# An attention and expert kernel on one core: tokens transposed once, router logits from extra matmul columns, values projected first, one power per chunk, places and gates turned on PE

## The chip, the core and the metric

The kernel runs on one core of one Trainium2 chip. The metric is the device time of one execution in microseconds, as the median of three runs. A profiled execution gives, beside its own time, a span (first to last instruction) and a trace of every engine: PE (matrix multiply), with its weight loads shown apart as PEld, DVE (vector), ACT (scalar and activation), POOL (GpSimd) and SP (which here only starts DMAs).

## The reference

The input x has 32 rows of 256 tokens with 128 features (shape 32 x 256 x 128). With xn the normalised x (mean 0, variance 1 over the features, no weights), the result is x + attention(xn) + block(xn). All weights are float32.

```python
def attention(x):                        # 16 heads of 8, over the 256 tokens of a row
    q, k, v = heads(x @ Wq), heads(x @ Wk), heads(x @ Wv)
    qc, kc = q - q.mean(-1, keepdims=True), k - k.mean(-1, keepdims=True)
    cov = einsum('bhsd,bhtd->bhst', qc, kc) / 8
    var = jnp.var(q, -1, ddof=1)[..., :, None] * jnp.var(k, -1, ddof=1)[..., None, :] / 8
    return merge(softmax(cov + var) @ v) @ Wo

def block(x):                            # here axis 0 (32) is the sequence, axis 1 (256) the batch
    h = layernorm(x, ln1_w, ln1_b)
    q, k, v = split(h @ in_proj_w.T + in_proj_b)
    a = causal_softmax(q @ k.T / sqrt(8)) @ v          # 16 heads of 8, over 32 positions
    x1 = x + a @ out_proj_w.T + out_proj_b
    h2 = layernorm(x1, ln2_w, ln2_b)
    gates, chosen = top_k(softmax(h2 @ router_w.T), 2)  # 8 experts
    return x1 + sum over the two chosen e of gate_e * gelu(h2 @ w1[e]) @ w2[e]
```

## The kernel before, in words

All loops are written out by hand, and each engine executes its instructions in the order in which the program lists them; waits between engines follow from the tiles that instructions share. Tiles of a pool are taken in rotation: the two PSUM pools u and w have four banks each.

**First stage** (first_rounds, L454, and last_rounds, L528). The 8192 tokens are cut into 16 chunks of 512, each as four tiles of 128 tokens. A chunk is 16 groups of 32 tokens that attend to each other (the causal attention of block). Round i of the loop at L464 holds pieces of several chunks, so that each engine finds work:

- measure(i+4), L269: statistics of the tokens on DVE, then on POOL the inverse root (a pow on 128x4), the bias -mean x root, and a second pow for the second normalisation, whose factor is r2.
- norms(i+3), L288: xn on ACT into zx (four activations), then zn = zx x r2 on POOL.
- turn_in(i+2), L303: PE transposes of zx (pta), copied by ACT into xnT for the second stage, and of zn (ptb), from which ACT makes hT with the weights ln1_w and ln1_b. POOL adds the output bias to zx.
- project_in(i+2), L313: keys (pk), from which ACT makes four masked copies kb (L320, one per group of heads), queries (pq, qT), and values (pv). The values go to DRAM (vald) and come back spread out (vb, L334).
- scores(i+1), L341: into four banks of the pool w, a mask matmul (L347) each and 64 small matmuls of 32x32 (L359).
- lessened and exponents, L371 and L377: DVE subtracts the maximum, bank by bank, and ACT exponentiates two banks at a time (h = 0 at the end of round i-1, h = 1 in round i).
- turn_weights, weigh, divide, L380 to L413: PE transposes the probabilities (ptp, to pT), multiplies them with the values (po), and DVE divides by the sums.
- turn_out and project_out, L415 and L419: transposes of the result (pto, oT), output projection px, x1 on DVE, statistics of x1, and on POOL the inverse root and the sum x + x1, which goes to DRAM (resd).
- normalise(i-1), L433: zx becomes the normalised x1 (POOL). turn_normed(i-2), L440, transposes it (ptc) and ACT makes h with ln2_w and ln2_b; logits(i-2), L444, multiplies h with the router (pl), and DVE copies the result to lg.

In rounds 3 to 5 set_second clears tiles of the second stage on POOL.

**Second stage** (step, L942). For each of 32 rows of 256 tokens, in two halves of the heads (64 units u, eight heads each), two heads per step: project (L554) multiplies 128 tokens of xnT, taken with a stride of 32 elements, with the three weight matrices (pp, 384 columns), ACT squares and copies, turn_qk transposes, scores_of (L594) computes scores twice, as sm for the row maxima (DVE, L622) and as sT for the exponentials (ACT, L625), weigh_head multiplies with the values, and divide_lessen, turn and close finish the row. A generator, route (L717), runs beside it: it yields after each of its instructions, and the step loop takes one to three of them at a time (L992): softmax, the two largest gates, the place of each token in its expert's blocks, then 128 indirect DMAs on POOL that scatter the tokens (L801). Places and gates are needed again by row; they are written to DRAM and read back in the other order (L792 to L798). In the middle of the stage the 71 expert blocks run (L870), and combine (L894) gathers their results during the second half.

Of the kernel before, what the change touches and what calls it, by code (L numbers as in the profile page):

```python
# [68 lines left out]
def block_kernel(  # L69
# [26 lines left out]
    xv = x.rearrange("s (i c k) e -> i c s (k e)", c=4, k=4)  # L96
# [7 lines left out]
    xnT = cp.tile([P, NCHUNK, 512], F32, name="xnT")  # L104
# [11 lines left out]
    posd = dp.tile([NB, SEQ, 2], I32, name="posd")  # L116
    gated = dp.tile([NB, SEQ, 2], F32, name="gated")
    xsd_views = dram_disjoint_views(xsd, 2 * NTILE)
    rv = resd.rearrange("s (i c k) e -> i c s (k e)", c=4, k=4)

    vec = cp.tile([P, 7], F32, name="vec")
    l1w, l1b, l2w, l2b = (vec[:, n:n + 1] for n in range(4))
# [5 lines left out]
    mhalf = cp.tile([P, 4, 1], F32, name="mhalf")  # L128
    wqkv = cp.tile([P, 3, P], F32, name="wqkv")
    wo = cp.tile([P, P], F32, name="wo")  # L130
    inT = cp.tile([P, 3, P], F32, name="inT")
    outT = cp.tile([P, P], F32, name="outT")
    rT = cp.tile([P, NE], F32, name="rT")

# [5 lines left out]
    def load(i):  # L140
        xt = ax.tile([P, 4, P], F32, tag="xt", name=f"xt{i}")
        for c in range(4):
            nc.sync.dma_start(xt[32 * c:32 * c + 32].rearrange("s k e -> s (k e)"), xv[i, c])
        return xt
# [13 lines left out]
    late = xnT[:, NCHUNK - 2:NCHUNK].rearrange("p i t -> p (i t)").rearrange("p (n m) -> p n m", m=P)  # L158
    ipw, opw, qkw, rw, bvs = late[:, 0:3], late[:, 3], late[:, 4:6], late[0:NE, 6], late[:, 7]
    qkT, ccen = zx[:, NTILE - 2:NTILE], zx[:, NTILE - 3]  # L160

    def loads():
# [7 lines left out]
        nc.scalar.dma_start(opw, out_proj_w)  # L170
        nc.scalar.dma_start(bout, out_proj_b.partition_broadcast(P))
# [3 lines left out]
        nc.sync.dma_start(rw, router_w)  # L175
# [5 lines left out]
    def set_in():  # L181
        nc.vector.tensor_scalar(bk4, cst[:, C_M4:C_M4 + 4], bk, None, ALU.mult)
        pt = bank_u([P, 4, P], "pt0")
        for n in range(3):
            nc.tensor.transpose(pt[:, n, :], ipw[:, n, :], ident)
        nc.tensor.transpose(pt[:, 3, :], opw, ident)
        nc.vector.tensor_copy(inT[:, 0:2, :], pt[:, 0:2, :])

        nc.vector.tensor_copy(
            inT[:, 2, :].rearrange("p (j g d) -> p j g d", j=4, g=4),  # L190
            pt[:, 2, :].rearrange("p (g j d) -> p j g d", j=4, g=4),
        )
        nc.vector.tensor_copy(outT, pt[:, 3, :])


        nc.vector.tensor_copy(bvs, bv.to_broadcast([P, P]))
        pbo = bank_u([P, P], "pbo")
        nc.tensor.matmul(pbo, bvs, outT, start=True, stop=True)
        nc.vector.tensor_tensor(bout, bout, pbo, ALU.add)

    def set_rest():
        pt = bank_w([P, 4, P], "pt1")
        nc.tensor.transpose(pt[:, 0, :], qkw[:, 0, :], ident)
        nc.tensor.transpose(pt[:, 1, :], qkw[:, 1, :], ident)
        nc.tensor.transpose(pt[:, 2, 0:NE], rw, ident[0:NE, 0:NE])
        nc.vector.tensor_copy(qkT, pt[:, 0:2, :])
        nc.vector.tensor_copy(rT, pt[:, 2, 0:NE])
# [3 lines left out]
        nc.vector.tensor_copy(wqkv[:, 0:2, :], pb)  # L211

# [29 lines left out]

    def set_values(n):
        nc.gpsimd.memset(vs[n].rearrange("p j k g d -> p (j k g) d")[:, :, HD:HD + 1], 1.0)
        nc.gpsimd.memset(vbs[n], 0.0)
# [9 lines left out]
    xts, rss, nrm, mvs, zns, hTs, qTs, kbt, scs, prs, pTs, wps, os, oTs, x1s, h2s = ({} for _ in range(16))  # L255

    def stats(src, tag, i, bufs=2):

        st = a2.tile([P, 4, 6], F32, tag="st", name=f"st{tag}{i}")
        mv = a2.tile([P, 4, 2], F32, tag=f"mv{tag}", name=f"mv{tag}{i}")  # L260
# [3 lines left out]
        rs = a2.tile([P, 4, 1], F32, tag=f"rs{tag}", name=f"rs{tag}{i}")  # L264
        nc.gpsimd.tensor_scalar(rs, mv[:, :, 1:2], EPS, None, ALU.add)
        nc.gpsimd.tensor_tensor(rs, rs, mhalf, ALU.pow)
        return mv, rs

    def measure(i):  # L269


        mv, rs = stats(xts[i], "a", i)
        nb = a2.tile([P, 4, 1], F32, tag="nb", name=f"nb{i}")
        nc.gpsimd.tensor_tensor(nb, mv[:, :, 0:1], rs, ALU.mult)
        nc.gpsimd.tensor_scalar(nb, nb, -1.0, None, ALU.mult)
        r2 = a2.tile([P, 4, 1], F32, tag="r2", name=f"r2{i}")
        nc.gpsimd.tensor_tensor(r2, rs, rs, ALU.mult)
        nc.gpsimd.tensor_tensor(r2, r2, mv[:, :, 1:2], ALU.mult)
        nc.gpsimd.tensor_scalar(r2, r2, EPS, None, ALU.add)
        nc.gpsimd.tensor_tensor(r2, r2, mhalf, ALU.pow)  # L280
        nrm[i] = rs, nb, r2
# [6 lines left out]
    def norms(i):  # L288
        rs, nb, r2 = nrm.pop(i)
        for k in range(4):  # L290
            nc.scalar.activation(
                tokens(i)[:, k, :], xts[i][:, k, :], AF.Identity, bias=nb[:, k, :], scale=rs[:, k, :]
            )
# [9 lines left out]
    def turn_in(i):  # L303

        nc.scalar.copy(
            xnT[:, i, :].rearrange("p (c k s) -> p k c s", c=4, k=4),
            transposed(tokens(i), "a", i).rearrange("p (k c s) -> p k c s", k=4, c=4),
        )
        hTs[i] = a2.tile([P, 512], F32, tag="hT", name=f"hT{i}")
        nc.scalar.activation(hTs[i], transposed(zns.pop(i), "b", i), AF.Identity, bias=l1b, scale=l1w)  # L310
        nc.gpsimd.tensor_tensor(tokens(i), tokens(i), bout.unsqueeze(1).to_broadcast([P, 4, P]), ALU.add)

    def project_in(i):  # L313
        hT = hTs.pop(i)
        pk = bank_w([P, 512], f"pk{i}")
        nc.tensor.matmul(pk, inT[:, 1, :], hT, start=True, stop=True)  # L316
# [5 lines left out]
        nc.tensor.matmul(pq, inT[:, 0, :], hT, start=True, stop=True)  # L322
        qTs[i] = a2.tile([P, 512], F32, tag="qT", name=f"qT{i}")
        nc.scalar.activation(qTs[i], pq, AF.Identity, bias=bq, scale=1.0)
        pv = bank_u([P, 4, 4, 32], f"pv{i}")
        for k in range(4):
            nc.tensor.matmul(pv[:, :, k, :], hT[:, k * P:(k + 1) * P], inT[:, 2, :], start=True, stop=True)
        nc.scalar.copy(
            vs[i % 2].rearrange("p j k g d -> p (j k g) d")[:, :, 0:HD],
            pv.rearrange("p j k (g d) -> p (j k g) d", d=HD),  # L330
        )
        nc.sync.dma_start(vald[i], vs[i % 2].rearrange("p j k g d -> p j (k g d)"))
# [86 lines left out]
    def project_out(i):  # L419

        oT = oTs.pop(i)
        px = bank_w([P, 4, P], f"px{i}")
        for k in range(4):
            nc.tensor.matmul(px[:, k, :], oT[:, k * P:(k + 1) * P], outT, start=True, stop=True)  # L424
        x1 = x1s[i] = a2.tile([P, 4, P], F32, tag="x1", name=f"x1{i}")
        nc.vector.tensor_tensor(x1, px, tokens(i), ALU.add)
        mvs[i], rss[i] = stats(x1, "c", i)
        xt = xts.pop(i)
        nc.gpsimd.tensor_tensor(xt, xt, x1, ALU.add)
        for c in range(4):  # L430
            nc.sync.dma_start(rv[i, c], xt[32 * c:32 * c + 32].rearrange("s k e -> s (k e)"))

    def normalise(i, eng=nc.gpsimd):  # L433
        x1, mv, rs = x1s.pop(i), mvs.pop(i), rss.pop(i)
        for k in range(4):
# [4 lines left out]
    def turn_normed(i):  # L440
        h2s[i] = a2.tile([P, 512], F32, tag="h2", name=f"h2{i}")
        nc.scalar.activation(h2s[i], transposed(tokens(i), "c", i), AF.Identity, bias=l2b, scale=l2w)

    def logits(i):  # L444
        pl = bank_u([P, 4, NE], f"pl{i}")
        h2 = h2s.pop(i)
        for k in range(4):
            nc.tensor.matmul(pl[:, k, :], h2[:, k * P:(k + 1) * P], rT, start=True, stop=True)
        nc.vector.tensor_copy(lg[:, 4 * i:4 * i + 4, :], pl)
# [4 lines left out]
    def first_rounds():  # L454
        loads()
        nc.vector.memset(mhalf, -0.5)
        measure(0)
        nc.gpsimd.tensor_copy(identb, ident)
        nc.gpsimd.tensor_copy(causalb, cst[:, C_CAUSAL:C_CAUSAL + 32])
        norms(0)  # L460
        set_in()
        measure(1)
        set_values(0)
        for i in range(-2, NCHUNK):  # L464
# [21 lines left out]
            if chunk(i + 2):  # L486
                project_in(i + 2)
            if i == NCHUNK - 1:
                project(0, 0)
# [6 lines left out]
            if i == -2:  # L496
                set_rest()
                set_values(1)
                nc.gpsimd.memset(zero, 0.0)
            if 3 <= i < 3 + NV:  # L500
                set_second(i - 3)
            if chunk(i + 3):
                norms(i + 3)
            if chunk(i + 4):
                measure(i + 4)
# [3 lines left out]
            if chunk(i - 1):  # L509
                normalise(i - 1)  # L510
            if chunk(i + 1):
                scores(i + 1)
            if chunk(i - 2):
                turn_normed(i - 2)
# [10 lines left out]
            if chunk(i - 2):  # L525
                logits(i - 2)

    def last_rounds():  # L528
# [5 lines left out]
        yield turn_normed(n - 1)  # L534
        yield project_out(n)
        yield logits(n - 1)
        yield normalise(n, nc.vector)
        yield turn_normed(n)
        yield logits(n)
# [5 lines left out]
    xs_all = xnT.rearrange("p i (b s) -> p (i b) s", s=NB)  # L545
    NU = 2 * NB
    pps = {}
    ot, qas, kas, exs, pos, oas, res = {}, {}, {}, {}, {}, {}, {}
# [5 lines left out]
    def project(s, ti):  # L554
# [3 lines left out]
            pp.rearrange("p n m -> p (n m)"), xs_all[:, ti * P:(ti + 1) * P, s],  # L558
# [4 lines left out]
        nc.scalar.activation(sq, pqk, AF.Square, scale=1.0 / math.sqrt(HD - 1))  # L563
        qk = qkts[s % NQ][:, ti].rearrange("p n g m r -> p (n g m) r")
        nc.scalar.copy(qk[:, :, 0:HD], pqk)
        pps[s, ti] = pp, sq

    def project_rest(s, ti):
# [4 lines left out]
        nc.scalar.copy(vo[:, :, 0, 0:8], pi[:, :, 0])  # L573
        qk = qkts[s % NQ][:, ti].rearrange("p n g m r -> p (n g m) r")
        nc.vector.tensor_reduce(qk[:, :, HD:HD + 1], sq, AX.X, ALU.add)
        nc.vector.tensor_copy(vo[:, :, 1, 8:16], pi[:, :, 1])
# [139 lines left out]

    def route():  # L717
# [3 lines left out]
        oh1, oh2 = r_tile("oh1", NTILE, NE), r_tile("oh2", NTILE, NE)  # L721
        yield nc.vector.tensor_reduce(m, lg, AX.X, ALU.max)
# [61 lines left out]
        yield nc.vector.tensor_tensor(a, a, n8[:, 0:1, :].to_broadcast(all8), ALU.add)  # L784
        posi = r_tile("posi", NTILE, 2, dt=I32)
# [235 lines left out]
```

## Time and profile before

| | |
|---|---|
| median of 3 runs | 991.37 us (991.09 to 992.39) |
| the profiled execution | 992.8 us, its span 991.0 us |
| mean granted clock of PE in it | 0.976 of full speed |
| busy in the span | PE 940.2, PEld 679.0, DVE 706.3, ACT 655.1, POOL 561.9 us |
| first stage | to about 285 us |
| second stage, first half; experts; second half | about 290 to 565; 565 to 705; 705 to 986 us |

The page gives the span in 40 equal slices, with the busy share of each engine in tenths and the clock that PE was granted. Lines of groups read: line, engine, operation, output from input, shapes, count; busy us, mean ns of one; idle time of the engine before them, and what ended it. Lines of the timeline read: start in us, length, engine, line, operation, tiles, shapes, count, and in brackets an idle time and its releaser. PE's instructions overlap, so that the distance between starts is what one costs in a row of them. A float32 matmul is two instructions, a transposition one.

### The profile page before, as it was taken

The page shows a single profiled execution, that of the slowest core. Times are in us where ns is not written, and L with a number is a line of the kernel's source. Part 1 is how long each engine was busy: PE and PEld are TensorE (multiplying, and loading weights), DVE is VectorE, ACT ScalarE, POOL GpSimd, SP SyncE. Part 2 cuts the span into 40 slices and gives each one's busy share as a digit, 9 for nine tenths or more (in the row PEclk, how much of TensorE's full clock was granted, in tenths as well). Part 3 has the DMA queues.
Part 4 walks back from the last instruction along what each step waited for, and adds up shares of the span by engine and source line. Part 5 has one row for each costly group of instructions (what it writes and reads, how often), then busy time and mean ns, then how long its engine had stood idle before and what let it go on. Part 6 is the DMA issues. An engine that isn't in the chain of part 4 may idle for free.

```text
span 991.0 us, 32300 instructions
## 1 busy us (share of the span) xinstructions
PE 940.2 (95%) x13107; PEld 679.0 (69%) x13107; DVE 706.3 (71%) x1638; ACT 655.1 (66%) x1362; POOL 561.9 (57%) x725
## 2 busy tenths in 40 slices
PE   4788999989789999999999999999999999999998
PEld 2567777777666666666666689999866666666664
DVE  2477578667589999888888834444588888888882
ACT  4687878877446666666666665555666666676664
POOL 5468787785310002777777123333387888888870
PEclk9798999999889999999999999999999999999999
DMA  3344434422031000541111134444222321121220
GB/s 100 108 132 125 134 120 139 140 60 68 21 102 35 2 2 15 59 111 55 55 53 54 52 117 135 133 134 136 76 60 63 81 69 36 39 68 52 55 60 22
DMA packets 87747, 76.32 MB, mean 77 GB/s; under 512 B 32840, under 2 KB 70864, under 8 KB 87600
## 3 DMA queue, kind: packets, MB, share of 16 engines
q1 hardware_dynamic: 74736, 48.03, 17.4%
q0 software_dynamic: 11600, 26.10, 8.5%
q8 instruction: 103, 1.69, 0.7%
q10 hardware_dynamic: 1264, 0.14, 0.1%
q14 instruction: 44, 0.36, 0.1%
HBM read 33.98 MB, written 40.24 MB: 75 GB/s over the span
## 4 chain that ended last, share of the span: by engine, by line
PE 86%; DVE 7%; issue 2%; POOL 2%; ACT 1%; DMA 0%; ACTq 0%; DVEq 0%; SPq 0%; POOLq 0%
PE sm L610 26%; PE pav L634 13%; PE pe L854 6%; PE pp L557 6%; PE ph L845 6%; PE pqk L584 3%; PE ptp L300 2%; PE sT L616 2%; PE pt L653 2%; PE sc L359 2%; DVE pr L375 2%; PE px L834 2%; PE pk L316 2%; PE px L424 2%; PE py L687 2%
## 5 line engine op out<-in xcount | busy, mean ns | idle before, releaser
L625 ACT ACTIVATE ex<-sT 128x512 f32<-128x512 f32 x512 | 277.7, 595 | 179.0 <-PE sT L616 179.0
L622 DVE TENSOR_REDUCE mt<-sm 128x2 f32<-128x512 f32 x512 | 329.0, 686 | 73.6 <-PE sT L616 67.7
L610 PE MATMUL sm<-ka,qa 32*128 32x256 f32 x2048 | 292.4, 402 | 3.5 <-DVE mt L622 3.5
L616 PE MATMUL sT<-qa,ka 32*128 32x256 f32 x2048 | 291.0, 400 | 0.0
L610 PEld LDWEIGHTS sm<-ka,qa 32*128 32x128 f32 x2048 | 177.4, 185 | 81.0 <-issue 38.1
L616 PEld LDWEIGHTS sT<-qa,ka 32*128 32x128 f32 x2048 | 176.4, 184 | 2.6 <-issue 1.7
L801 POOL DMA_INDIRECT xsd<-zx,posi x128 | 122.9, 960 | 81.4 <-DVE posi L789 42.7
L905 POOL DMA_INDIRECT yg<-ysd,posb x128 | 122.1, 954 | 43.0 <-issue 31.5
L634 PE MATMUL pav<-ex,va 128*32 128x256 f32 x2048 | 137.2, 385 | 0.0
L859 POOL DMA_DIRECT2D ysd<-ye x71 | 48.2, 679 | 115.0 <-DVE ye L858 89.1
L634 PEld LDWEIGHTS pav<-ex,va 128*32 128x32 f32 x2048 | 53.8, 109 | 64.2 <-issue 24.0
L854 PEld LDWEIGHTS pe<-w,ge 128*128 128x128 f32 x568 | 74.5, 192 | 4.2 <-ACT ge L847 0.7
L854 PE MATMUL pe<-w,ge 128*128 128x128 f32 x568 | 74.9, 275 | 0.3 <-ACT ge L847 0.3
L845 PE MATMUL ph<-xT,w 128*128 128x256 f32 x284 | 73.3, 381 | 0.0
L557 PE MATMUL pp<-wqkv,xnT 128*128 128x384 f32 x128 | 65.6, 595 | 0.8 <-DVE mt L622 0.8
L858 DVE COPY ye<-pe 128x256 f32<-128x256 f32 x71 | 30.1, 424 | 50.8 <-PE pe L854 50.8
L837 ACT ACTIVATE xT<-px,vec 128x256 f32<-128x256 f32 x71 | 39.9, 563 | 35.8 <-PE px L834 35.8
L847 ACT ACTIVATE ge<-ph 128x512 f32<-128x512 f32 x71 | 42.4, 597 | 21.1 <-PE ph L845 21.1
L378 ACT ACTIVATE pr<-pr 128x1024 f32<-128x1024 f32 x32 | 33.8, 1058 | 34.0 <-DVE pr L375 33.9
L374 DVE TENSOR_REDUCE mx<-sc 128x16 f32<-128x512 f32 x64 | 43.4, 678 | 17.3 <-PE sc L359 17.3
L828 DVE COPY w<-wall 128x512 f32 x71 | 30.4, 429 | 33.3 <-issue 31.9
L845 PEld LDWEIGHTS ph<-xT,w 128*128 128x128 f32 x284 | 48.5, 191 | 4.1 <-ACT xT L837 0.4
(170 smaller groups left out, 1663.0 us busy)
## 6 DMA issues: line engine op xcount, KB each, us to landing
xb<-xsd SPq DMA_DIRECT2D x71, 128.0 KB, 2.1
ysd<-ye POOLq DMA_DIRECT2D x71, 128.0 KB
xsd<-zero SPq DMA_DIRECT2D x10, 852.0 KB
vald<-v SPq DMA_DIRECT2D x16, 288.0 KB, 2.3
vb<-vald SPq DMA_DIRECT2D x64, 72.0 KB, 3.0
xt<-in_L_attn_x_dram SPq DMA_DIRECT2D x64, 64.0 KB, 2.0
resd<-xt SPq DMA_DIRECT2D x64, 64.0 KB, 1.7
res<-resd SPq DMA_DIRECT2D x32, 128.0 KB, 3.3
```

The source lines that it names most:

```text
L374: nc.vector.tensor_reduce(mx, s, AX.X, ALU.max)
L557: nc.tensor.matmul(pp.rearrange("p n m -> p (n m)"), xs_all[:, ti * P:(ti + 1) * P, s], wqkv.rearrange("p n m -> p (n m)"), start=True, st ...
L610: nc.tensor.matmul(sc[:, i, :], qas[u][r:r + 32, i * P:(i + 1) * P], kas[u][r:r + 32, h, :], start=True, stop=True,)
L616: nc.tensor.matmul(sc[:, i, :], kas[u][r:r + 32, h, i * P:(i + 1) * P], qas[u][r:r + 32, :], start=True, stop=True,)
L622: nc.vector.tensor_reduce(mts[y // 8 % 2][:, :, o:o + 1], sc, AX.X, ALU.max, negate=True)
L625: nc.scalar.activation(exs[y], sc, AF.Exp, scale=1.0 / HD)
L634: nc.tensor.matmul(pos[u][32 * j:32 * j + 32, :], vaugs[s % NV][:, ti, 4 * j + 2 * g + h, :], exs[8 * u + 4 * h + j][:, ti, :], start=(h = ...
L801: yield nc.gpsimd.indirect_dma_start(xsd_views[n * NTILE + k], bass.IndirectOffsetOnAxis(ap=posi[:, k, n:n + 1], axis=0), zx[:, k, :], None,)
L845: nc.tensor.matmul(ph[:, f, :], wb[n][0][:, f * P:(f + 1) * P], xT, start=True, stop=True)
L854: nc.tensor.matmul(pe[:, j, :], ge[:, f, j * P:(j + 1) * P], w2b[:, f, :], start=(f == 0), stop=(f == 1))
L859: nc.gpsimd.dma_start(ysd[n * BLK:(n + 1) * BLK].rearrange("(p j) h -> p j h", j=2), ye)
L905: yield nc.gpsimd.indirect_dma_start(yg[s][:, ti, n, :], None, ysd, bass.IndirectOffsetOnAxis(ap=gt["posb"][:, s, ti, n:n + 1], axis=0),)
```

## The change

The chunks are cut differently (a row of x is now addressed by half, part and chunk, L96), so that the eight tiles of a row lie in a regular pattern. Then:

1. Only zn is transposed. znT keeps it as it comes; ln1_w goes into the projection weights (set_in), ln1_b into the projection biases, and the second stage, which needs xn, multiplies its projections by 1/r2 instead: pointer scales on ACT and DVE in project and project_rest. The factors are turned from tokens in chunk order to tokens in row order by small PE matmuls with the identity (by_position, scale_back).
2. For the second stage ACT copies each row's 256 tokens together (gather), so that project reads them without a stride.
3. The logits come from additional columns: 8 in the output projection, and 32 (8 used) in the values' projection; the mean, the inverse root and the bias rows are applied to all 64 tiles at once at the start of route, in five POOL operations. turn_normed and logits are gone. Values are projected ahead of keys and queries, in two halves; px also takes two banks.
4. The two powers of a chunk become one on 128x8, most of its small operations move to DVE, and measure moves ahead of project_out. The inverse root of x1, the sum for the residual and its DMAs move to a piece of their own (residual) after norms.
5. Places and gates are turned by PE (turn_places) within route; the 12 DMAs are gone.
6. The set-up is reordered: norms of chunks 0 and 1 on DVE, more of set_in and set_rest for the folded weights, POOL's clearing of the second value tile later.

```diff
+    def turn_in(i):
+        nc.scalar.copy(znT[:, i, :], transposed(zns.pop(i), "b", i))
...
+    def values_in(i):
+        zT = znT[:, i, :]
+        v = vs[i % 2]
+        invert(i)
+        for h in range(2):
+            pv = bank_u([P, 5, 2, 32], f"pv{i}_{h}")
+            for k in range(2):
+                o = (2 * h + k) * P
+                nc.tensor.matmul(pv[:, :, k, :], zT[:, o:o + P], inV, start=True, stop=True)
+            nc.scalar.copy(
+                v[:, :, 2 * h:2 * h + 2].rearrange("p j k g d -> p j (k g) d")[:, :, :, 0:HD],
+                pv[:, 0:4].rearrange("p j k (g d) -> p j (k g) d", d=HD),
+            )
+            t = slice(4 * i + 2 * h, 4 * i + 2 * h + 2)
+            nc.vector.tensor_tensor(
+                lg[:, t, :], pv[:, 4, :, 0:NE], rall[:, t].unsqueeze(2).to_broadcast([P, 2, NE]), ALU.mult
+            )
...
     def project_in(i):
+        zT = znT[:, i, :]
+        values_in(i)
         pk = bank_w([P, 512], f"pk{i}")
-        nc.tensor.matmul(pk, inT[:, 1, :], hT, start=True, stop=True)
+        nc.tensor.matmul(pk, inT[:, 1, :], zT, start=True, stop=True)
...
     def measure(i):
-        mv, rs = stats(xts[i], "a", i)
+        mv, _ = stats(xts[i], "a", i)
+        sm = a2.tile([P, 8, 1], F32, tag="sums", name=f"sums{i}")
+        nm = a2.tile([P, 4, 1], F32, tag="nm", name=f"nm{i}")
+        nc.vector.tensor_scalar(sm[:, 0:4], mv[:, :, 1:2], EPS, None, ALU.add)
+        nc.vector.tensor_scalar(nm, mv[:, :, 0:1], -1.0, None, ALU.mult)
+        nc.vector.reciprocal(sm[:, 4:8], sm[:, 0:4])
+        nc.vector.tensor_tensor(sm[:, 4:8], sm[:, 4:8], mv[:, :, 1:2], ALU.mult)
+        nc.vector.tensor_scalar(sm[:, 4:8], sm[:, 4:8], EPS, None, ALU.add)
+        rr = a2.tile([P, 8, 1], F32, tag="rr", name=f"rr{i}", bufs=3)
+        nc.gpsimd.tensor_tensor(rr, sm, mhalf, ALU.pow)
         nb = a2.tile([P, 4, 1], F32, tag="nb", name=f"nb{i}")
...
     def project_out(i):
         oT = oTs.pop(i)
         x1 = x1s[i] = a2.tile([P, 4, P], F32, tag="x1", name=f"x1{i}")
+        for h in range(2):
+            px = bank_w([P, 2, P + NE], f"px{i}_{h}")
+            for k in range(2):
+                o = (2 * h + k) * P
+                nc.tensor.matmul(px[:, k, :], oT[:, o:o + P], outX, start=True, stop=True)
+            nc.vector.tensor_tensor(
+                x1[:, 2 * h:2 * h + 2, :], px[:, :, 0:P], tokens(i)[:, 2 * h:2 * h + 2, :], ALU.add
+            )
+            l = lg[:, 4 * i + 2 * h:4 * i + 2 * h + 2, :]
+            nc.vector.tensor_tensor(l, l, px[:, :, P:P + NE], ALU.add)
         mvs[i], rss[i] = stats(x1, "c", i)
...
+    def by_position(to, by):
+        for h in range(2):
+            for c in range(4):
+                r = slice(32 * c, 32 * c + 32)
+                nc.tensor.matmul(to[r, h, :], by[r, 32 * h:32 * h + 32], ident[r, r], start=True, stop=True)
...
+    def gather(s):
+        xs[s] = bh.tile([P, SEQ], F32, tag="xs", name=f"xs{s}", bufs=2)
+        nc.scalar.copy(xs[s].rearrange("p (h c n) -> p h c n", h=2, c=4), xs_all[:, :, :, :, s])
...
-            pp.rearrange("p n m -> p (n m)"), xs_all[:, ti * P:(ti + 1) * P, s],
+            pp.rearrange("p n m -> p (n m)"), xs[s][:, ti * P:(ti + 1) * P],
...
-        nc.scalar.copy(qk[:, :, 0:HD], pqk)
+        nc.scalar.activation(qk[:, :, 0:HD], pqk, AF.Identity, scale=rpos[:, 0, ti, s:s + 1])
```

Within a round of first_rounds the order is now:

```diff
             if chunk(i + 2):
                 project_in(i + 2)
+            if chunk(i + 4):
+                measure(i + 4)
             if i == NCHUNK - 1:
+                gather(0)
+                gather(1)
                 project(0, 0)
                 project_rest(0, 0)
...
+                norms(1)
+                set_out()
                 set_rest()
+            if 3 <= i < 3 + NV:
+                set_second(i - 3)
+            if 2 <= i + 3 < NCHUNK:
+                norms(i + 3)
+            if chunk(i - 1):
+                residual(i - 1)
+            if chunk(i + 2):
+                bias_out(i + 2)
+            if i == -1:
                 set_values(1)
...
-            if chunk(i - 2):
-                turn_normed(i - 2)
...
-            if chunk(i - 2):
-                logits(i - 2)
+            if i == NCHUNK - 3:
+                scale_back()
```

In the second stage the gather of row u/2 + 3 stands at the end of each even unit, on ACT behind the two exponentials of that step.

220 lines of the change are left out of this document (118 added, 102 removed).

## The prediction

> **What bounds the kernel now.** I read the page's forty slices first, then the busy times of longer stretches, the waits of the first stage, its timeline, and the groups of weight loads.
>
> ```profile
> PE   4788999989789999999999999999999999999998
> ...
> PEclk9798999999889999999999999999999999999999
> ```
>
> ```profile
> 60.00:240.00 180.00, 164.43 (x3917) 129.62 (x3892) 124.17 (x351) 141.88 (x241) 137.48 (x215) 0.94 0.38 115
> ```
>
> The second fence gives PE, PEld, DVE, ACT, POOL, then the granted clock. From slice 12 (300 us) on PE is full: what is saved on PE there is saved outright. Before that, no engine is: PE is busy 91%, ACT 79%, POOL 76%, DVE 69%, with the clock at times reduced. So a chain of waits binds the first stage, and I looked for it in one undisturbed chunk (150 to 168 us):
>
> ```profile
> 150.98 1.90 PE L359 MATMUL sc<-kb,qT 32*32 32x128 f32 x128
> ...
> 165.11 1.82 PE L359 MATMUL sc<-kb,qT 32*32 32x128 f32 x119
> ```
>
> ```profile
> 156.15 1.06 ACT L378 ACTIVATE pr<-pr 128x1024 f32<-128x1024 f32 x1 [1.30 <-DVE pr L375]
> 157.16 0.59 ACT L305 COPY xnT<-pta 128x512 f32<-128x512 f32 x1
> 157.64 0.79 ACT L310 ACTIVATE hT<-ptb,vec 128x512 f32<-128x512 f32 x1
> 158.89 1.08 ACT L383 COPY pT<-ptp 128x512 f32<-128x512 f32 x2 [0.46 <-PE ptp L300]
> 160.53 1.06 ACT L378 ACTIVATE pr<-pr 128x1024 f32<-128x1024 f32 x1 [0.57 <-DVE pr L375]
> 161.50 0.57 ACT L417 COPY oT<-pto 128x512 f32<-128x512 f32 x1
> 161.96 2.79 ACT L320 ACTIVATE kb<-pk,bk,cst 128x512 f32<-128x512 f32 x4
> ```
>
> The chunk takes 14.13 us from sc to sc. Its links: sc ends at 152.88; DVE, still busy with the next token statistics, starts the first maximum 0.39 late (153.27); four maximum and subtract pairs with two divisions between them run to 160.44; the second exponential starts at 160.53, oT at 161.50, the four kb at 161.96 to 164.75, and sc 0.36 after the last kb. The cause of this last link is the rotation of four PSUM banks in the pool w: pk, px and the four sc are taken in turn, so the third sc bank is pk's, free when kb has read it; two of the four mask matmuls (L347, 0.215 each) come after it. In seven other chunks sc also follows the last kb by 0.35 to 0.36. PE's work of the chunk fits between these links.
>
> **The change, part by part.**
>
> *Removed PE work (16 chunks).* The transposes pta and ptc and the logits pl: 0.48, 0.6 and 0.95 us per chunk in that timeline, 2.0 in all; pv's wider rows (160 for 128 columns, 8 instructions at 0.107 to 0.133) give back 0.2, px's 0.05. All three removed pieces stand between the end of sc and the first ptp (152.9 to 158.2), where PE has to wait for the maxima and the exponential anyway. Without them ptp can start at 0.1 after the first exponential, 3.85 after sc's end, as at 260.06 in the last chunk; pto waits for the second division, 5.5 after it. So I price this removal at **no gain by itself**; its cover is the DVE chain, and without that the 1.8 net would count (a rival below).
>
> *DVE moved and added.* measure(i+4) goes ahead of project_out, into the idle time of 2.94 before L426. Added per chunk: five small operations and two reciprocals (0.16 to 0.25 each by the rows of rT L207 and nb L275, some 1.4), two logit products and two additions (0.18 each as lg L449), x1 in two halves (2 x 0.42 for 0.69). DVE then ends its statistics some 1.3 us ahead of sc, and the first maximum starts 0.16 before sc's end shows, as in the chunks where it waited (240.09 against 240.25): **-0.55** per chunk.
>
> *ACT reordered.* The values are now copied ahead of kb, in two halves. Two 128x256 copies follow each other by 0.28 (264.63 to 264.91): 0.56, at most 0.76 by their durations: **+0.56**, on the chain. px takes two banks instead of one, so pk's bank is now the second sc bank and three mask matmuls come behind it: **+0.21**. Together a chunk goes from 14.13 to 14.35 by terms; from the on-time chunks (13.4, at 45.8 and 223.9) the same terms give 14.2, which I take.
>
> *Chunks that were disturbed.* From the first sc (33.52) to the last (254.30) the 15 intervals take 220.8. Two are 17.2 and 16.7: POOL's memsets (2.6 us each) ahead of zn made ptb wait. POOL loses the pow of 1.04, five small ones (1.1) per chunk; the joint pow on 8 columns costs between 1.04 (fixed) and 2.07 (by element), off the chain at both ends; so these two become ordinary. Others are 15.1 to 15.95 by a half clock:
>
> ```profile
> 182.04:185.45 3.41, 1.76 (x41) 1.60 (x29) 3.05 (x8) 2.00 (x3) 3.16 (x7) 0.97 0.33 82
> 185.45:188.86 3.41, 3.41 (x77) 3.00 (x76) 2.10 (x5) 1.36 (x2) 3.16 (x6) 0.53 0.15 41
> ```
>
> Cut into stretches of 3.41 us, the clock halves after stretches with PE busy 1.40 to 2.49 of 3.41; others of 2.01 to 2.63 were not followed by it. The thinner PE work makes such stretches commoner, I think in 6 chunks of 10. But pk has 1.0 us of slack before kb (it ends 7.9 after sc, kb starts at 8.9), so the 1.7 us that a half-speed stretch costs PE shows with 0 to 0.7: 0.2 on average. New sum: first interval 13.1, thirteen of 14.2, the fourteenth, without kb, 15.5 (15.95 now), 14 x 0.2: 216.0, **-4.8** (bounds -12 to +6).
>
> The Trainium skill, "TensorE: Matmul & The Clock Gate" (Why this matters for your kernels), warns of PE gaps of over about 3 us, since one idle window returns the clock to half. It speaks against a change that thins PE out; by its letter the gaps of 2 us here would cost nothing, but the fence shows a half clock after a stretch that was half busy, so the trace decides.
>
> *Start.* Chunk 0's ptb comes 2.3 earlier (one pow and pta less), but values come first there too at half clock (8 x 0.27), and chunk 1's ptb stands on PE behind set_out and set_rest, which now wait for measure(2), the norms and three 1.02 us broadcast copies on DVE: about 25.8 for 26.14; then values ahead of kb (+2.1, less 0.6 of a shorter copy): sc at 34.7, **+1.2** (-3 to +4).
>
> *Hand-over, 256 to 289.* DVE's 14 maxima (0.62 each) carry most of it. The last ptc (0.8) and pl (1.18) before the first sT go; two gathers on ACT ahead of the first pp, with px behind it, add 0.9: **-1.0** (-4 to +3).
>
> *Second stage, pp.* The gathered tokens make pp's stationary operand contiguous.
>
> ```profile
> L557 PEld LDWEIGHTS pp<-wqkv,xnT 128*128 128x128 f32 x36 | 9.3, 305 | 6.0 <-issue 6.0
> L584 PEld LDWEIGHTS pqk<-cst,qk 128*128 128x128 f32 x76 | 8.9, 141 | 0.0
> L687 PEld LDWEIGHTS py<-wo,boT 128*128 128x128 f32 x36 | 5.4, 191 | 1.4
> ```
>
> Of the 128x128 loads only pp's is strided (128 bytes between columns) and it takes 305 where py's takes 191. A pp stands 0.85 on PE (424.53 to 425.38), and two passes of 384 columns at pk's rate (0.43 per 512) need 0.64; the excess of 0.21 holds the first load. I take the difference of the loads, 0.114, for 52 of 64 pp (in the other 12, up to 400 us, DVE binds: busy 95.17 of 100): **-5.9**; bounds 0 and -13.4 (64 x 0.21). The Trainium skill, "SBUF — State Buffer" (Door 1: The DMA port swizzle), says that accesses which leave a 16-byte line pay a penalty; it gives no figure, but it is the same cause.
>
> ACT gains 32 gathers (128x256, 0.28 to 0.6 if the stride costs it too) and pointer scales on 192 operations (ka 0.49 against qa 0.38: 0.11 each). Hidden: ACT waits for sT 175.6 us in all, 0.7 at each step; uncovered, it would be up to 35.
>
> *PE transposes of places, gates, scales.* 5 x 16 small instructions, 12 ns each by po (64 in 0.77) to 26 (103 ns loads, four side by side), with changes of tile shape: **+1.5** (0.6 to 3). The 12 removed DMAs on SP, with 8-byte elements, have nobody on the path waiting: 0.
>
> *Routing.* Five POOL operations (1.3 each, early enough) ahead and one DVE cast less push five DVE operations of 0.69 past the point where three are issued per step; scatters end some 5 us later, with 20 to spare before the experts: **+1.1** (-1 to +2).
>
> **Sum:** +1.2 - 4.8 - 1.0 - 5.9 + 1.5 + 1.1 = -7.9. The span 991.0 becomes 983.1, the profiled execution's 992.8 becomes 984.9; it lay 1.4 over the median of 991.4, so I predict **983.5**, with its own range 977 to 989. The measurement can tell 0.2% (2 us) from no change.
>
> **Rivals.**
> *PE was the bound.* For: 91% busy. Then 14 chunks give 1.9 each, -26.6 in place of -4.8: 961.7. Against: sc follows kb's end by 0.36. Chance 0.10.
> *The gather gives back what pp gains.* If the 0.21 is a change of tile shape and not the load, or ACT's additions delay a few ex, the -5.9 goes: 989.4; for it, py and pt also show 0.1 of excess. Chance 0.15.
> *The clock.* Without any half clock the change would save 10.7 (7.9 + 2.8). If thinner PE work halves the clock in every chunk, in the part from pto to kb where slack is short, each pays up to 1.7: 14 x 1.7 = 23.8, so 1004.5. It decides from 0.77 us per chunk on. For: the fence above; against: pk's slack. Chance 0.20.
> The forecast has 0.55. That the change does not do what it says would show as pta or ptc still there; I give it nothing.
>
> Range: 970 to 999 leaves out the first rival and half of the third. Faster 0.68 (forecast, first rival, a little of the second), same 0.12, slower 0.20.
>
> **What would show it.** Right: sc to sc 14.0 to 14.6 in undisturbed chunks, sc within 0.7 of the last kb, the maximum released by PE sc, ptb no longer released by zn, pp's loads at 185 to 200 and its pair 0.7 to 0.76 on PE. Wrong: sc to sc under 13.3 (PE was the bound), more than half of the stretches before 250 us at clock 0.5, or ACT with no idle time before ex in the second stage.

## The result, and the profile after

The kernel after takes **1001.20 us** (median, 1000.78 to 1004.11) beside 991.74 for the kernel before on the same chip (991.09 to 992.39): ratio **1.0102**, 95% interval [1.0081, 1.0122]. It is 1% slower; the forecast was 983.5. The profiled execution took 1004.11, its span 1002.3 (before: 992.8 and 991.0), so 11.3 us are to be found between the two traces.

The page's first rows and the window of the first stage, kernel after:

```profile
PE   4788878887769999999999999999999999999998
...
PEclk9899999999779999999999989999999999999999
```

```profile
60.00:240.00 180.00, 150.12 (x3660) 113.09 (x3659) 139.48 (x477) 128.30 (x233) 120.71 (x147) 0.94 0.39 117
```

TensorE has 14 us less to do in this window (150.12 for 164.43) at the same granted clock of 0.94, and the stage is no shorter. VectorE has 15 us more. TensorE's row of slices is thinner in six of the slices 5 to 12.

Placed by marks that both traces have (us; difference in the last column):

| from, to | before | after | |
|---|---|---|---|
| start to the first sc | 33.5 | 35.0 | +1.5 |
| first sc to the 16th sc | 220.8 | 221.4 | +0.6 |
| 16th sc to the first ex of the second stage (hand-over) | 36.1 | 42.3 | +6.2 |
| first ex to the 36th unit's pp | 271.8 | 273.6 | +1.8 |
| that pp to the experts' first px | 7.6 | 9.7 | +2.1 |
| px to the experts' first pe | 4.06 | 5.14 | +1.1 |
| first pe to the end | 417.1 | 415.1 | -2.0 |

**The chunk.** A clean one takes 14.66 us from sc to sc, where it took 14.13. TensorE's rows of the timeline around one (start, duration, what ended the idle time):

```profile
137.29 1.90 PE L419 MATMUL sc<-kb,qT 32*32 32x128 f32 x128
...
149.47 0.38 PE L407 MATMUL sc<-causalb,identb 128*128 128x512 bf16 x1
150.77 1.25 PE L407 MATMUL sc<-causalb,identb 128*128 128x512 bf16 x3 [0.92 <-ACT kb L388]
151.94 1.90 PE L419 MATMUL sc<-kb,qT 32*32 32x128 f32 x128
```

ScalarE in the same chunk:

```profile
145.95 1.06 ACT L438 ACTIVATE pr<-pr 128x1024 f32<-128x1024 f32 x1 [1.07 <-DVE rall L330]
146.91 0.57 ACT L477 COPY oT<-pto 128x512 f32<-128x512 f32 x1
147.38 0.65 ACT L370 COPY v<-pv 128x256 f32<-128x256 f32 x2
147.91 2.81 ACT L388 ACTIVATE kb<-pk,bk,cst 128x512 f32<-128x512 f32 x4
```

And VectorE:

```profile
145.77 0.17 DVE L330 RECIPROCAL rall<-rr 128x4 f32<-128x4 f32 x1
147.79 0.45 DVE L375 TENSOR_TENSOR lg<-pv,rall 128x16 f32<-128x16 f32 x2 [1.85 <-ACT v L370]
148.24 0.29 DVE L302 BATCH_NORM_STATS2 sta<-xt 128x6 f32<-128x128 f32 x1
...
150.58 0.17 DVE L320 TENSOR_SCALAR sums<-sums 128x4 f32<-128x4 f32 x1
150.66 0.42 DVE L488 TENSOR_TENSOR x<-px,zx 128x256 f32<-128x256 f32 x1
151.00 0.16 DVE L492 TENSOR_TENSOR lg<-lg,px 128x16 f32<-128x16 f32 x1
...
151.41 0.16 DVE L492 TENSOR_TENSOR lg<-lg,px 128x16 f32<-128x16 f32 x1
```

The last kb ends at 150.72, and sc starts 1.22 after it, where it followed by 0.36 before. One mask matmul could run early; the second waits for kb's bank, the third and the fourth for px's two banks, which VectorE frees with its two lg, at 151.16 and 151.57 (starts at 151.00 and 151.41, 0.16 each). VectorE is late with these because it sat idle for 1.85 us, waiting with the logit product for ScalarE's value copy, and then did a later chunk's statistics (148.24 to 150.75) ahead of them. Over the window this wait is 22.2 us in 12 places, the largest of VectorE. The pair of marks for a chunk now reads: sc's start to the first maximum 1.74 (2.29 before), maximum to oT 7.88 (8.23), oT to kb 1.00 (0.46), kb 2.81, kb to sc 1.22 (0.36): the two gains of 0.55 and 0.35 are less than the two losses of 0.54 and 0.86.

The 0.86 has two halves. The masks of the chunk of the kernel before are this row:

```profile
163.99 1.19 PE L347 MATMUL sc<-causalb,identb 128*128 128x512 bf16 x4
```

They take 0.38 each and start 0.215 apart, so the third starts at 164.42, before the last kb ends (164.75), and only the fourth comes behind it, at 164.80. In the kernel after three come behind kb: two more are 0.43, and VectorE's late release of px is the other 0.43. In one chunk of e2 below, where px was free in time, sc follows kb by 0.79 with three masks behind it. So the four banks of the pool w are not taken in a fixed rotation, as the text ahead of the prediction has it: kb's bank comes last in the kernel before and second in the kernel after.

**The hand-over.** TensorE's rows, kernel after:

```profile
264.11 0.44 PE L351 MATMUL pto<-cst,o 128*128 128x128 f32 x2 [0.48 <-DVE o L473]
267.57 1.65 PE L639 MATMUL pp<-wqkv,xs 128*128 128x384 f32 x2 [3.03 <-ACT xs L630]
269.01 2.02 PE L487 MATMUL px<-outX,oT 128*128 128x136 f32 x8
```

and VectorE's, some 20 us later:

```profile
286.83 2.05 DVE L505 TENSOR_SCALAR zx<-x,mvall,rsall 128x128 f32<-128x128 f32 x4 [1.09 <-POOL rsall L308]
288.80 4.87 DVE L705 TENSOR_REDUCE mt<-sm 128x2 f32<-128x512 f32 x8
```

pp, first in TensorE's order, waits 3.03 us for the first gather, which stands on ScalarE behind the exponential and oT; px and the rest wait behind pp. The clock then halves (windows of 4 us; the granted clock is the third number from the end):

```profile
264.00:268.00 4.00, 0.86 (x3) 0.63 (x4) 1.34 (x3) 2.62 (x5) 0.00 (x0) 0.87 0.00 0
268.00:272.00 4.00, 4.00 (x16) 3.39 (x16) 2.01 (x9) 1.17 (x5) 0.00 (x0) 0.50 0.00 0
```

VectorE then waits 1.09 for POOL's inverse root before it normalises the last chunk, takes 2.05 for that (before: no wait, and 1.15 by the next row), and eight maxima are queued behind it.

```profile
282.14 1.15 DVE L436 TENSOR_SCALAR zx<-x,mvc,rsc 128x128 f32<-128x128 f32 x4
```

Over the whole hand-over the mean granted clock is 0.78, where it was 0.91 before. How much of the 6.2 us is the lower clock and how much the waits themselves, no run separates; e2 below wins 2.8 us of them at 0.76.

**The second stage.** The loads, in the window 400 to 560 of the kernel after, as in the prediction's fence (mean ns of one is the number behind the busy time):

```profile
L770 PEld LDWEIGHTS py<-wo,boT 128*128 128x128 f32 x36 | 5.4, 191 | 2.4
L639 PEld LDWEIGHTS pp<-wqkv,xs 128*128 128x128 f32 x36 | 5.4, 188 | 6.3 <-issue 5.3 <-DVE mt L705 0.6 <-DVE posb L806 0.3
```

pp's load is 188 ns for 305, as forecast. The unit (pp to pp) that TensorE bounds fell from 8.607 to 8.530 on average. Units come in two kinds by turns: 8.72 and 8.493 before, 8.615 and 8.445 after, so one kind won 0.105 and the other only 0.048.

### The profile page after: what moved, and what is told of

Its sections match the earlier page's. It is cut to its first block, busy times and chain, and to the rows that moved or that the text cites. A ratio compares the mean times of both kernels' runs of the same rounds, so it can differ in the third digit from the quotient of the medians.

```text
span 1002.3 us, 32003 instructions
## 1 busy us (share of the span) xinstructions
PE 924.1 (92%) x12940; PEld 649.6 (65%) x12940; DVE 736.7 (74%) x1818; ACT 666.8 (67%) x1370; POOL 543.3 (54%) x634
## 5 line engine op out<-in xcount | busy, mean ns | idle before, releaser
L693 PE MATMUL sm<-ka,qa 32*128 32x256 f32 x2048 | 299.0, 404 | 4.1 <-DVE mt L705 1.9
L693 PEld LDWEIGHTS sm<-ka,qa 32*128 32x128 f32 x2048 | 182.6, 186 | 83.9 <-DVE mt L705 28.2
L639 PE MATMUL pp<-wqkv,xs 128*128 128x384 f32 x128 | 60.7, 557 | 5.9 <-ACT xs L630 3.0
L322 POOL TENSOR_TENSOR rr<-sums,mhalf 128x8 f32<-128x8 f32 x16 | 26.7, 1672 | 70.8 <-DVE sums L320 70.8
L941 ACT ACTIVATE ge<-ph 128x512 f32<-128x512 f32 x71 | 42.4, 597 | 22.2 <-PE ph L939 22.2
```

What stands on the lines that cost most here:

```text
L639: nc.tensor.matmul(pp.rearrange("p n m -> p (n m)"), xs[s][:, ti * P:(ti + 1) * P], wqkv.rearrange("p n m -> p (n m)"), start=True, stop=True,
L693: nc.tensor.matmul(sc[:, i, :], qas[u][r:r + 32, i * P:(i + 1) * P], kas[u][r:r + 32, h, :], start=True, stop=True,)
```

## The experiments

All but one are edits of the kernel after. Four of them (e4, e6, e7, e8) ran on a chip on which every kernel, before too, took some 240 us more. By the trace of e4 some 165 us of them fall in the stretch in which POOL issues its scatters (TensorE is busy 31 us of 160 there) and some 70 in the second half of the second stage, where it issues its gathers. A gain in us is a smaller ratio on this chip. What I read in these traces lies ahead of the scatters, but for the unit of e8, which lies between the two stretches. The kernel after did not run on this chip.

**e1: the order on VectorE.** The statistics go ahead of the projections in:

```
-            if chunk(i + 2):
-                project_in(i + 2)
             if chunk(i + 4):
                 measure(i + 4)
+            if chunk(i + 2):
+                project_in(i + 2)
```

> The changed kernel, with measure(i+4) put ahead of project_in(i+2) in the round, so that DVE takes the statistics of the tokens while it would wait for ACT to copy the values. Theory DVE order: in the changed kernel the mask matmuls wait for px's second bank, which DVE frees only after it waited 1.85 us for the copy of the values and then took 2.5 us of statistics; with the statistics first, x1 and its logits come some 1.8 us earlier, sc follows the last kb by about 0.75 instead of 1.22, and a chunk takes 14.1 to 14.3 us from sc to sc instead of 14.66: 6 us in 14 chunks, ratio to the kernel before 1.003 to 1.005. Theory clock (fewer PE instructions, more stretches at half clock): the order on DVE does not matter, chunks stay at 14.6 to 14.7, ratio 1.010.

993.79 us, ratio 1.0041 [1.0020, 1.0062]. The clean chunk fell from 14.66 to 13.78, more than expected. VectorE and TensorE, one chunk:

```profile
131.39 0.17 DVE L330 RECIPROCAL rall<-rr 128x4 f32<-128x4 f32 x1
131.67 0.26 DVE L375 TENSOR_TENSOR lg<-pv,rall 128x16 f32<-128x16 f32 x2
131.84 0.42 DVE L488 TENSOR_TENSOR x<-px,zx 128x256 f32<-128x256 f32 x1
```

```profile
132.79 0.81 PE L407 MATMUL sc<-causalb,identb 128*128 128x512 bf16 x3
133.91 0.38 PE L407 MATMUL sc<-causalb,identb 128*128 128x512 bf16 x1 [0.31 <-ACT kb L388]
134.22 1.90 PE L419 MATMUL sc<-kb,qT 32*32 32x128 f32 x128
```

The product no longer waits, x follows it at once, and sc starts 0.36 after the last kb (131.05 + 2.81 = 133.86) again. Three masks run early and only one stands behind kb, so kb's bank comes last again: the exchange brought back both halves of the 0.86. The same operations in another order: the order is the cause. The kernel after shows it itself in its 13th and 14th intervals, which have no statistics left to do and take 13.79. The product waits 1.84 and 1.85 us there too, so the wait costs a chunk nothing by itself; wait and statistics together do.

**e6: why the product waits.** In `values_in` the logit product is issued before the value copy of the same tile (two statements exchanged).

> The kernel after with one exchange: VectorE's product for the logits is issued ahead of ScalarE's value copy from the same PSUM tile; the statistics stay where they are. Theory: VectorE waited 1.85 us per chunk for ScalarE's read of that tile and not for the matmul; the product then comes that much earlier, the statistics and the residual sum follow, and a clean chunk falls from 14.66 to between 13.8 and 14.2: ratio 1.003 to 1.006. Rival: it waited for the matmul, or the value copy now waits for VectorE and delays the key copies as much: 1.009 to 1.011.

Ratio 1.0062 [1.0042, 1.0083], a little above the theory's range, which the interval holds; 7.6 us over the kernel before; clean chunk 13.92. VectorE's waits, 60 to 240 us:

```profile
DVE lg L371 <- PE pv L369: 5.3, 12, 0.7
```

22.2 us of waiting have become 5.3, now for the matmul. So VectorE had waited for ScalarE's read of the tile pv, of other columns than it needs, because that read was issued first. By the trace this one exchange of two reads shortens the first stage as e1 does: 215.0 us from the first sc to the 16th, 214.8 in e1, 221.4 in the kernel after. The total does not show all of it: the kernel after was 9.5 us over the kernel before, on another chip, so 1.9 us are seen of 6.4. Where the rest went stays open.

**e5: the clock.** Sixteen more transposes per chunk that nobody reads, between the scores and the first weighing, to keep TensorE busy.

> The changed kernel with 16 more transposes of the identity per chunk on PE, between sc and the multiplication with the values, 1.75 us in all at full clock, about what the change removed there; nothing reads them. Theory DVE order: PE waits in that place anyway, so a chunk gains 0 to 0.3 us, ratio 1.010 to 1.014. Theory clock: the filled stretch keeps the clock up, the stretches at half clock before 240 us get fewer and the time falls, ratio 1.003 to 1.008. Theory that PE is the bound of the first stage: 1.75 us more per chunk, 28 us, ratio 1.038.

1004.18 us, ratio 1.0147 [1.0109, 1.0186], by its median a little above the theory's range.

```profile
60.00:240.00 180.00, 162.63 (x3850) 124.19 (x3849) 138.69 (x470) 126.66 (x232) 120.73 (x147) 1.00 0.38 115
```

The granted clock is 1.00 for 0.94, TensorE does 12.5 us more work, and the clean chunk takes 14.81 for 14.66. Half-clock stretches in the chunks were not what cost the time, and neither was TensorE's work: 16 more instructions at full speed cost 0.15 us a chunk. That a busier array keeps its clock is what the Trainium skill says in "TensorE: Matmul & The Clock Gate" (Part 1); in these chunks it was worth nothing.

**e2: the gathers of the hand-over.** `gather(0)` and `gather(1)` move from the last chunk to two chunks earlier.

> The changed kernel, with the first two gathers two rounds earlier (end of round 13, when the last tokens have been transposed). Theory gather in line: at the hand-over PE stands 3.0 us with pp at the head of its queue, waiting for two gathers on ACT that come behind the exponential and oT, and falls to half clock through that; with the gathers early, pp runs in the wait for oT as in the kernel before, and the first sT comes 4 to 6 us earlier: ratio 1.004 to 1.006. Theory that the hand-over is late for the normalisation of chunk 15 and the root on POOL: the first sT gains 1 us at most, ratio 1.009 to 1.010.

997.15 us, ratio 1.0069 [1.0029, 1.0108], a little above the range, which the interval holds. pp no longer waits for xs; the hand-over takes 39.5 for 42.3.

**e7: the normalisation of the last chunk.** `normalise(n, nc.vector, ...)` becomes `normalise(n, nc.gpsimd, ...)`.

> The kernel after with one operation on another engine: the normalisation of the last chunk goes to POOL, like those of the other chunks. Theory: in the hand-over VectorE waits 1.09 us there for POOL's inverse root and then takes 2.05 us, ahead of maxima that TensorE waits for; both go: 2 to 3 us, ratio 1.007 to 1.0085. Rival: TensorE has to wait for the maxima's banks anyway: ratio 1.0095 to 1.0105.

Ratio 1.0075 [1.0043, 1.0107], too wide to tell the theories apart; in us it is 9.3 over the kernel before. The trace can tell: the hand-over takes 37.8 for 42.3, though pp still waits 2.4 for the gather, and no maximum stands behind POOL's 3.13 us for the same work. As in e6, the total shows less than the trace ahead of the scatters.

**e3: POOL's additions to the routing.** The five new POOL operations are issued without turns between them.

> The changed kernel, with the five POOL operations at the start of the routing issued together and not one per step. Theory places late: the scatters begin 21.7 us later than in the kernel before, because four more steps of the routing and the later single cast hold back the places, they run on POOL one after another for 160 us, and the experts' entry waits for the last one; with five steps less (1.2 units of 9 us) the scatters begin about 10 us earlier and the experts' entry loses its 3 us: ratio 1.006 to 1.008. Theory that the entry to the experts is late only because everything before it is: ratio 1.010.

998.94 us, ratio 1.0109 [1.0067, 1.0152]: no gain by the median, but the interval is too wide to exclude one of 2 to 3 us. The first scatter stands 103.5 us after the first ex for 111.6, and the last one starts at 559.1, 16.6 us ahead of the experts' first px (11.0 in the kernel after). The way from the 36th unit's pp over px to the first pe takes 13.8 us for 14.8 (11.6 before). In e2 it takes 11.9, with the last scatter only 9.2 us ahead of px. So the scatters' delay is not what made the experts' entry late.

**e4: three of these together** (e1, e2, e3).

> The kernel after with three changes at once: statistics of a later chunk ahead of the projections in, the first two gathers two chunks earlier, the five new POOL operations of the routing without turns between them. If the losses stand in different places (VectorE's order in the chunks 6.1, the gathers in the hand-over 3.3, POOL's turns nothing), the gains add up: ratio to before 1.0000 to 1.0015. Rival: the hand-over takes back what the chunks win, because the last chunk's own chain sets it: 1.003 to 1.005.

Ratio 0.9992 [0.9976, 1.0007], by its median just below the range. The gains add up; the time is that of the kernel before within the interval.

**e9: with e7 as a fourth.**

> The kernel after with four changes: statistics ahead of the projections in, first gathers two chunks earlier, POOL's five routing operations without turns between them, and the last chunk's normalisation on POOL. Theory: hand-over (last sc to first ex, 42.3 us in the kernel after, 36.1 before) loses 2.8 by the gathers and 4 to 4.5 by the normalisation, the chunks lose 6: ratio to before 0.9955 to 0.9980. Rival: in the hand-over the two stand one behind the other and the second gives nothing more: 0.9985 to 1.0005.

989.27 us beside 988.97, ratio 1.0000 [0.9982, 1.0019]: the theory's number is missed, and the rival's fits, but not for the rival's reason. Its hand-over is as the theory has it, 34.4 us (35.5 to 35.9 in the three kernels that follow, which share it). But from the first ex to the 36th unit's pp it takes 275.3 us, where the kernel after took 273.6 and e3 272.0. What the fourth edit wins ahead of the first ex is given back in the stretch behind it, where VectorE is busy 95.3 us of 100. That this stretch has a fixed amount of VectorE work which simply starts earlier is my reading; no run isolates it.

**e10: VectorE relieved.** As e9, and ScalarE scales both halves of the second stage's values:

```
-        nc.vector.tensor_scalar(vo[:, :, 1, 8:16], pi[:, :, 1], r, None, ALU.mult)
+        nc.scalar.activation(vo[:, :, 1, 8:16], pi[:, :, 1], AF.Identity, scale=r)
```

> As the run with four changes, and both halves of the second stage's values are scaled by ScalarE, none by VectorE (0.28 us per unit in the kernel after, 0.22 before). Theory: in the units up to about 400 us VectorE is the bound (busy 90%), so some 12 units win 0.2 to 0.4 each: 2 to 4 us less than the run with four changes, ratio lower by 0.002 to 0.004. Rival: ScalarE's longer row of operations makes the exponentials late in every unit: higher by 0.001 to 0.004.

985.80 us, ratio **0.9958** [0.9936, 0.9979]: faster than both kernels. The stretch from the first ex to the 36th unit's pp takes 272.9 for 275.3, and the later unit 8.502 for 8.530. The later units are 8.615 and 8.389 by turns, as in e8 below, where VectorE copies these values without a scale in 0.22: there the pointer scale, 0.28 us for 0.22 on VectorE, had cost every second unit 0.055. In the early units, which VectorE bounds, this run takes all 0.28 us off VectorE and not only the 0.06 that the change had added, so what the scale alone had cost there is not isolated.

**e11: values behind keys.** As e9, with the value copies behind kb and qT.

> As the run with four changes, and ScalarE copies the first phase's values behind the keys and queries, as the kernel before does; the matmuls and the logits stay ahead. Theory: the two copies' 0.53 us stand on the path from oT to the key copies to sc, so each of some 14 chunks wins 0.3 to 0.55 (a clean chunk 13.2 to 13.5 in place of 13.78): 4 to 8 us, ratio lower by 0.004 to 0.008. Rival: the copies then stand ahead of pT, and the weighted sums and divisions come as much later: within 0.001 of the run with four changes.

1006.82 us, ratio 1.0168 [1.0141, 1.0194]: both theories are wrong, by over 15 us. A clean chunk takes 15.11. TensorE, one chunk:

```profile
140.22 0.60 PE L351 MATMUL ptp<-cst,pr 128*128 128x128 f32 x4
142.26 0.66 PE L351 MATMUL ptp<-cst,pr 128*128 128x128 f32 x4 [1.44 <-ACT qT L397]
```

ScalarE, which reads the banks of pq and pv there:

```profile
141.50 0.71 ACT L397 ACTIVATE qT<-pq,vec 128x512 f32<-128x512 f32 x1
142.07 0.67 ACT L379 COPY v<-pv 128x256 f32<-128x256 f32 x2
```

The pool u has four banks: two pv, pq and the first ptp take them. With the values behind qT both pv hold theirs until after 142.07; the second ptp waits for ScalarE and starts 0.05 after qT has read pq (142.21), so it was given pq's bank. In the kernel after the second ptp follows the first without a wait. The mask matmuls and sc are queued behind that ptp. The values have to be read first because a bank is wanted next.

**e8: the gather alone, in the kernel before.**

> The kernel before with one part of the change alone: each sequence's tokens are gathered into contiguous columns by ScalarE, the first two of them two chunks before the end of the first phase, and the projection loads from there. Theory: the load falls by 0.11 us, and in the 52 or so units that TensorE bounds this is won in full: 4.5 to 6 us, ratio 0.9940 to 0.9955. Rival: the unit is set by something beside TensorE's own work, as the kernel after has it (a unit shorter by 0.04 to 0.08 us only): 1.5 to 3.5 us, ratio 0.9965 to 0.9985. Second rival: the gathers' 0.6 us on ScalarE push the exponentials: 1.000 to 1.002.

Ratio 0.9962 [0.9940, 0.9984], 4.9 us less than before: between theory and rival by the ratio, in the theory's range by us; the unit fell from 8.607 to 8.502 (8.616 and 8.389 by turns), so the load alone is worth 0.105 a unit. One part of the change, put into the kernel before without the rest, makes it faster.

**e12: the load alone, in e9.**

> As the run with four changes, but without gathers: each projection of the second stage loads its tokens with a stride of 128 bytes, as before (in another order within a tile, so the output's order differs; only its time is looked at). Theory: the load alone makes the unit that TensorE bounds, 8.607 before and 8.530 after: 0.077 times some 50 units, 4 us more, ratio higher by 0.003 to 0.005. Rival: the shorter unit comes from elsewhere and the gathers cost as much as they save: within 0.0015.

This run takes the tokens of a tile in another order than the output wants them and so does not compute the kernel's result; only its time counts. 993.21 us, ratio 1.0043 [1.0026, 1.0060], so 3.9 us more than e9.

```profile
L638 PEld LDWEIGHTS pp<-wqkv,znT 128*128 128x128 f32 x36 | 9.3, 304 | 6.0 <-issue 6.0
```

The load is 304 ns again and the unit 8.607 again: beside VectorE's pointer scale the stride costs 0.077 us per unit, without it 0.105 (e8).

## Why the prediction was wrong

*Start, +1.2:* right (+1.5).

*Chunks, -4.8:* wrong, +0.6. The step that failed is "measure(i+4) goes ahead of project_out, into the idle time of 2.94". The first half held: the maximum was on time, released by sc, and gained its 0.55. But a queue has no idle time that is independent of what stands in it. The new product in front of the statistics waited 1.85 us for another engine's read of its tile (I priced it at 0.18 and did not ask whom it waits for), the idle time went into that wait, and the statistics pushed the residual sum, which holds the banks that sc needs. For the banks I had +0.21 and never asked when px is freed: +0.86. The reading behind the 0.21 was wrong as well: "two of the four mask matmuls (L347, 0.215 each) come after it" is one in the trace of the kernel before, because the banks do not come in rotation, so three masks behind kb are 0.43 more, and the late px another 0.43. The value copies' +0.56 was right (0.54). In the right order (e1) a chunk takes 13.78, less than the 14.2 forecast, with sc 0.36 behind kb: no 0.21 at all. The disturbed chunks went as forecast in part: the two of 17.2 and 16.7 are gone.

*Hand-over, -1.0:* wrong, +6.2, and outside my bounds of -4 to +3. "Two gathers on ACT ahead of the first pp ... add 0.9" counted their duration, not that ScalarE reaches them only behind an exponential and oT, nor that everything on TensorE is queued behind pp (e2: 2.8). And I did not price normalise(15) on VectorE at all, which in the new order waits for POOL and stands before eight maxima (e7: 4.5).

*pp, -5.9:* the mechanism was right, and nearly the size. The load fell by 0.117, and alone it takes 0.105 off the unit (e8): over some 52 units 5.5 us. In the kernel after only 0.077 of it is left, 4.0 us (e12: 3.9), because VectorE's pointer scale takes 0.028 back (e10). The prediction names the 16-byte line as the cause of the stride's price; no run here shows which cause it has.

*Transposes of places, gates, scales, +1.5, and routing, +1.1:* together the rest of the second stage lost 7.0: between the first ex and the end the trace lost 3.0 net, and pp had won 4.0. The first scatter was late not by 5 but by 21.7 us (8.4 from what lies ahead of the first ex, 13.4 from the routing's longer order, of which e3 takes back 8); this did not make the experts' entry late (e2, e3). Among what cost is the VectorE copy turned into a pointer scale (e10), which I had among ScalarE's hidden additions and did not see on VectorE. The 3.2 us at the experts' start (7.6 to 9.7, 4.06 to 5.14) go with a half clock there (0.78 in the window 580 to 590) after a TensorE wait of 1.9 us for VectorE's maxima, 1.55 before. In e2 and e12 the same wait is not followed by it, and they lose 0.3. What decides this stays open.

*Rivals.* "PE was the bound" is excluded by e5. "The gather gives back what pp gains" did not happen in the units. "The clock" named 1004.5, close to the measured time, and was wrong as a mechanism: from 60 to 240 us it is 0.94 in both kernels, and 1.00 in e5 with the loss intact. The clock is lower in the hand-over (0.78 for 0.91), where the prediction did not look for it, behind waits that the order of the queues makes. A rival's number that fits is no proof of the rival.

Sum of the misses: 5.4 in the chunks, 7.2 in the hand-over, 1.9 for pp with the scale that eats into it, 4.4 in the rest of the second stage, 0.3 at the start: 19.2, the distance from -7.9 to +11.3.

## What to carry to other kernels

Before you place an operation into an engine's idle time, write down whom each new instruction in front of it waits for, and which buffer the instructions behind it hold: an operation of 0.2 us can move a chunk by 0.9. When two engines read one PSUM tile, issue first the read of the engine whose queue others wait for, and let the bank that is wanted next be read first. Price the junction of two stages by the queue order of its first instructions, and try a change's parts alone: here the gather by itself, or the whole with five edits of order and engine, was faster, and the change as it stood was slower.

## What was not expected of the hardware

- A joint pow on 128x8 takes POOL 1672 ns, where 128x4 took 1.04 us: by these two an estimate of 0.41 us fixed and 0.158 per column.
- ScalarE pays for a scale by pointer: sq 0.39 to 0.47, qk 0.37 to 0.47, va 0.26 to 0.33 us. The Trainium skill, "ScalarE: Activation LUTs" (What ACT_TABLE_LOAD costs), has about 93 ns for each pointer operand; the rows show 0.07 to 0.10. VectorE pays 0.06 for va.
- A gather of 128x256 with steps between its elements takes ScalarE 0.57 to 0.64 us, where a copy of this size out of PSUM (qa) takes 0.37.
- The four normalisations of 128x128 took VectorE 2.05 us in the kernel after for 1.15 before, for no reason that a run isolates.
